# A recurrent recommender on one core: keys of eight steps gathered as whole rows and stored sorted, and seven sums moved from VectorE to GpSimd

## The chip, the core and the metric

The kernel runs on one core of one Trainium2 chip, in one launch. The metric is device time in microseconds, the median of three timed executions. Five engines work side by side and wait for each other only through semaphores: TensorE (PE in the profile) multiplies matrices, VectorE (DVE) and ScalarE (ACT) work elementwise, GpSimd (POOL) works elementwise more slowly and issues gathers, and SyncE (SP) issues plain transfers between the memory outside the core (DRAM in the code) and the core's own memory. Each engine takes its instructions strictly in the order of the program.

## What is computed

There are 1024 users, 100 time steps and 128 channels. Cut to what matters:

```
h[t]    = GRU(h[t-1], x[t])                         # 100 steps; keys[t] = h[t]
s[t]    = relu-MLP([key, item, key - item, key * item])   # one number per user and step
attn    = softmax over t of s[t], where mask[t] == 1
pooled  = sum over t of attn[t] * keys[t]           # 1024 users x 128 channels
a[t, b] = pooled.T[:100][t, b]                      # channel t of the pooled row is the weight of step t
g[t]    = AUGRU(g[t-1], keys[t], a[t])              # a second pass over the 100 steps:
          r, u = sigmoid(W [g, key]);  c = tanh(W [g * r, key]);  u = a[t] * u
          g    = (1 - u) * g + u * c
score   = MLP([user, item, history sum, item * history sum, g[length - 1]])
```

The second pass can only start once the pooled rows are there, and those need the last GRU step.

## The kernel before, in words

The users lie along the free dimension, 512 to a half, two halves; the 128 channels lie along the partitions. The **first phase** (`gru_phase`) loops over the 100 GRU steps. Per step and half TensorE runs the gate matmuls (L588) and the matmuls of the score MLP (L770). VectorE turns each new state by 32x32 blocks into the tile `kt` (L655), which holds four steps in a row layout, and `store` (L667) writes each such group of four to DRAM. GpSimd weighs the same tiles by the softmax weights and adds them up: product `kw` (L699), sum `pooled` (L700), and a rescaling of the sum (L689) when the softmax maximum moves on. The softmax goes by blocks of steps; each block's scores come from the rows `s_b`, which SP writes from the MLP's output `mv` (L825) and which VectorE reads (L865).

Between the phases lies a stretch that this document calls **the passage**: the last softmax blocks, the last sums, the product of the first AUGRU weights (L1114, L1122, L1128), the first AUGRU state `h_all` (L1137), and the rest of the pooled sums over channels 4 to 31 of each block (`rest`, L1141 for half 0 on GpSimd, L1143 for half 1 on VectorE). The pooled rows are then stored (L1146), gathered sorted by length (`gather_weights`, L1186), masked (L1206), turned, stored (L1216) and read back step by step as the tiles `at` (`load_att`, L1228).

The **second phase** (`augru_phase`) runs with the users sorted by length, longest first, so that later steps work on fewer columns. A step of a half is `half_step` (L1279): TensorE opens the three gates with the key's part (L1264) and closes them with the state's part (L1268); ScalarE applies sigmoid (L1292, L1293) and tanh (L1276); VectorE forms `r` (L1300), the weighted `u` (L1305, which reads `at`), `rest` (L1308) and the new state (L1298, L1302). The two halves alternate.

The keys must therefore come sorted. Before the change the keys of steps 0 to 3 are gathered as whole rows of one user (`keys_d[0]`, L158). All others lie in DRAM as rows of 32 channels by eight steps, 1 KB each, and one gather (`load_row`, L186, issued at L193) fetches 128 of these rows, so that a half takes 16 gathers for eight steps. Steps 4 to 11 of half 0 are gathered in the passage into the pool `kx` (four at step 98, four just after the loop, eight at the end of the passage); those of half 1 at the start of the second phase (16 gathers, four at once and twelve spread over steps 1 and 2). `load_key` (L1232) turns them back into the key tiles (L1253).

The order of the work is written out by hand: each engine's and each queue's order is the order of the program text. SP's transfers and GpSimd's gathers go to two queues (q1 and q0 in the profile) that share 16 DMA engines.

Of the kernel before, what the change touches and what calls it, by code (L numbers as in the profile page):

```python
# [9 lines left out]
F32 = mybir.dt.float32  # L10
# [9 lines left out]
P = 128  # L20
B = 1024
T = 100
HB = 512
# [4 lines left out]
R = 32  # L28
# [22 lines left out]

G = 4
WHOLE = 1
READ = [G] * WHOLE + [2 * G] * ((T - WHOLE * G) // (2 * G))
READ += [T - sum(READ)] * (sum(READ) < T)
FIRST = [sum(READ[:q]) for q in range(len(READ))]

# [28 lines left out]
def kernel(ctx: ExitStack, tc: tile.TileContext, a: dict, out: bass.AP):  # L86
# [30 lines left out]
    keys_d = [  # L117
        dram.tile([B, n * P] if q < WHOLE else [NK * P, n * R], F32, name=f"keys_d{q}")
        for q, n in enumerate(READ)
    ]  # L120
    mask_d = dram.tile([T, B], BF16, name="mask_d")
    inv_d = dram.tile([B, 3], I32, name="inv_d")
    kc_d = dram.tile([2, P], I32, name="kc_d")
# [43 lines left out]
    def load_rows(q, i, width, tiles):  # L167

        n = READ[q]
        if q < WHOLE:  # L170
            r = rows[q, i] = tiles.tile([P, GH, n * P], F32, tag="once", name="rows")
            for g in range(GH):
                gather(r[:, g, :], keys_d[q], g, i)
                yield
            return

        parts, tag = (2, "kt") if tiles is kx else (1, "rows")
        some = [
            tiles.tile([P, KH // parts, n * R], F32, tag=tag, name="rows") for _ in range(parts)
        ]  # L180
        rows[q, i] = some
        for k in range(-(-width // R)):
            load_row(q, i, k)
            yield

    def load_row(q, i, k):  # L186
        some = rows[q, i]
        part, at = divmod(k, KH // len(some))
        r = some[part]
        if later.get("pace") is not None:  # L190

            nc.gpsimd.tensor_copy(r[:, at, 0:1], later["pace"])  # L192
        nc.gpsimd.indirect_dma_start(  # L193
            out=r[:, at, :],
            out_offset=None,
            in_=keys_d[q],
            in_offset=bass.IndirectOffsetOnAxis(ap=idx_k[:, k, i : i + 1], axis=0),
        )

    def all_of(steps):  # L200
        for _ in steps:
            pass

    def gru_phase(pools):
# [334 lines left out]
        class Half:  # L539
# [125 lines left out]
                    self.store(q)  # L665

            def store(self, q):  # L667
                row, part = divmod(q - WHOLE, 2)
                nc.sync.dma_start(
                    out=keys_d[WHOLE + row].rearrange("(k p) m -> p k m", p=P)[  # L670
                        :, self.ks, ts(part, G * R)
                    ],
                    in_=self.kt[q].rearrange("p k n c -> p k (n c)"),
                )
# [259 lines left out]
        def gather_early(n):  # L934
            for _ in range(n):
                next(more_early)


        late, again, early_from = 6, 24, 84
        for s in range(T):  # L940
# [5 lines left out]
            def loads():  # L946
# [6 lines left out]
                if s == T - AHEAD:  # L953
# [107 lines left out]
        stage()  # L1061
        exponents()
        take(T + 1)
        some(4, 5)

        def key(n, half):
# [73 lines left out]
        kept = halves[0].kt[q]  # L1140
        halves[0].pool(T, nc.gpsimd, rest)  # L1141
        for half in halves:
            half.pool(T, nc.vector, rest)  # L1143
            to = pooled_d[half.cols, :].rearrange("(k r) f -> r k f", r=R)
            for p in range(P // R):
                nc.sync.dma_start(  # L1146
                    out=to[:, :, ts(p, R)], in_=pooled[ts(p, R), half.ks, :]
                )
        halves[0].kt[q] = kept
        halves[0].store(q)  # L1150
        all_of(more_early)

    def augru_phase(pools, widths, alive):

# [378 lines left out]
        def spread(q):  # L1533


            ahead = 3 if widths[FIRST[q]] > HB // 2 else 4
            n = NH * -(-widths[FIRST[q]] // R)
            return spread_over(n, NH * (FIRST[q] - FIRST[q - 1] + 1 - ahead))
# [161 lines left out]
```

## Time and profile before

| | |
|---|---|
| timed executions | 1998.15, 1998.83 and 1998.97 us; median 1998.83 us |
| the profiled execution, its own time | 2015.4 us |
| its span, first to last instruction | 2013.5 us |
| mean granted TensorE clock | 0.995 |
| TensorE busy | 1982.8 us (98% of the span) |
| VectorE busy | 1674.2 us (83%) |
| ScalarE busy | 940.4 us (47%) |
| GpSimd busy | 1262.1 us (63%) |
| gathers at L193 | 218, mean 972 ns on GpSimd |

A time in a row of the timeline or of the chain is counted from the start of the span. A row has its start, its length, the engine, the line of the kernel, the operation with what it writes and reads, and in square brackets how long the engine sat idle before it and what ended that. "issue" there means that nothing the profile shows ended it. The rows themselves stand in the prediction.

### The profile page before, as it was taken

Reading aid. Unit: us, or ns where it says so; the run is one execution under the profiler, and the core shown is the slowest. Engines: PE = TensorE matmul, PEld = TensorE weight load, DVE = VectorE, ACT = ScalarE, POOL = GpSimd, SP = SyncE. Lnnn points to the kernel's source line nnn. Section 1 sums busy time; section 2 is a strip of 40 time slices with the busy share of each in tenths; the row PEclk is TensorE's granted clock in tenths of the full one; section 3 lists DMA queues with packets and bytes.
Section 4 is the critical chain, followed back from the end, with each engine's and each line's share of the span. In section 5 each row is a group of like instructions: output and inputs, shape, how many; then the busy total and the mean of one; then the engine's idle time right before and its main releaser. Section 6 shows DMA issues by size and latency. Waiting matters only on the chain.

```text
span 2013.5 us, 40927 instructions
## 1 busy us (share of the span) xinstructions
PE 1982.8 (98%) x15324; PEld 875.7 (43%) x15324; DVE 1674.2 (83%) x3036; ACT 940.4 (47%) x1689; POOL 1262.1 (63%) x1300
## 2 busy tenths in 40 slices
PE   9999999999999999999999999999699999999998
PEld 2333333333333333333333333334244556678997
DVE  7888998887888897888888898998477777888885
ACT  4445444444445454445445454455234444445553
POOL 0333939569796959495987767989553354445331
PEclk9999999999999999999999999999899999999999
DMA  4443333323334334333432333332443333333331
GB/s 124 98 117 100 98 107 107 105 84 90 107 115 108 108 117 122 109 115 105 126 101 80 99 107 92 107 107 83 126 136 93 95 110 98 94 104 95 81 81 35
DMA packets 244572, 205.59 MB, mean 102 GB/s; under 512 B 61811, under 2 KB 207068, under 8 KB 244364
## 3 DMA queue, kind: packets, MB, share of 16 engines
q1 hardware_dynamic: 231852, 170.31, 29.9%
q0 software_dynamic: 12224, 32.05, 5.7%
q8 instruction: 122, 2.00, 0.4%
q14 instruction: 86, 0.70, 0.1%
q10 hardware_dynamic: 288, 0.52, 0.1%
HBM read 146.75 MB, written 54.42 MB: 100 GB/s over the span
## 4 chain that ended last, share of the span: by engine, by line
PE 93%; DVE 2%; POOL 2%; another core or an unknown queue 1%; ACT 1%; issue 1%; DMA 0%; SPq 0%; DVEq 0%; ACTq 0%; POOLq 0%
PE ps L588 48%; PE pm L770 17%; PE ph L1268 4%; PE pr L1268 4%; PE pu L1268 4%; PE ph L1264 4%; PE pr L1264 4%; PE pu L1264 4%; POOL pooled L700 1%; PE last L737 1%; POOL kw L699 1%; PE pr L1359 0%; PE ph L1359 0%; POOL hist L574 0%
## 5 line engine op out<-in xcount | busy, mean ns | idle before, releaser
L588 PE MATMUL ps<-x,wih 128*32 128x512 f32 x4800 | 601.9, 592 | 0.0
L588 PE MATMUL ps<-hn,whh 128*32 128x512 f32 x4752 | 596.8, 592 | 0.0
L588 PEld LDWEIGHTS ps<-x,wih 128*32 128x32 f32 x4800 | 174.4, 110 | 342.6 <-issue 337.9
L588 PEld LDWEIGHTS ps<-hn,whh 128*32 128x32 f32 x4752 | 172.8, 110 | 339.1 <-issue 337.0
L600 ACT ACTIVATE r<-ps,brz 128x512 f32<-128x512 f32 x200 | 137.5, 687 | 381.9 <-PE ps L588 381.7
L573 POOL TENSOR_TENSOR xm<-x,m 128x512 f32<-128x512 f32 x200 | 233.5, 1168 | 66.9 <-DMA m<-mask_d 66.6
L574 POOL TENSOR_TENSOR hist<-hist,xm 128x512 f32<-128x512 f32 x200 | 257.7, 1288 | 15.7
L193 POOL DMA_INDIRECT rows<-keys_d,idx_k x218 | 211.9, 972 | 85.2 <-POOL rows L192 49.7
L700 POOL TENSOR_TENSOR pooled<-pooled,kw 128x512 f32<-128x512 f32 x192 | 245.0, 1276 | 15.0
L699 POOL TENSOR_TENSOR kw<-kt,e 128x512 f32<-128x512 f32 x192 | 206.3, 1074 | 69.0 <-DVE e L888 69.0
L621 ACT ACTIVATE ps<-ps,bih 128x512 f32<-128x512 f32 x198 | 131.1, 662 | 229.8 <-DVE ps L618 228.7
L770 PE MATMUL pm<-hn,wk 128*32 128x512 f32 x1200 | 214.9, 592 | 0.0
L770 PE MATMUL pm<-kq,wkq 128*32 128x512 f32 x1200 | 214.8, 592 | 0.0
L1276 ACT ACTIVATE c<-ph,bh 128x510 f32<-128x510 f32 (+57 forms) x174 | 88.1, 506 | 254.5 <-PE ph L1268 222.1
L608 DVE SCALAR_TENSOR_TENSOR u<-ps,bhh,r 128x512 f32<-128x512 f32 x198 | 147.5, 745 | 68.8 <-PE ps L588 66.6
L770 PE MATMUL pm<-mv,w 128*32 128x512 f32 (+1 forms) x808 | 194.9, 592 | 1.0 <-DVE e L869 1.0
L192 POOL COPY rows<-rest 128x1 f32<-128x1 f32 x186 | 34.9, 188 | 209.5 <-DVE rest L1308 205.5
L631 DVE TENSOR_TENSOR d<-hn,ps 128x512 f32<-128x512 f32 x198 | 136.1, 687 | 35.9 <-ACT ps L621 35.5
L618 DVE TENSOR_TENSOR ps<-ps,u 128x512 f32<-128x512 f32 x200 | 140.0, 700 | 25.2 <-remote 4.1
L632 DVE TENSOR_TENSOR d<-ps,d 128x512 f32<-128x512 f32 x198 | 136.9, 691 | 26.1 <-ACT ps L622 11.1
L642 ACT COPY hn<-ps 128x512 f32<-128x512 f32 x198 | 115.5, 583 | 91.6 <-DVE kq L637 89.9
L1298 DVE TENSOR_TENSOR pu<-pu,c 128x510 f32<-128x510 f32 (+57 forms) x173 | 81.8, 473 | 89.7 <-ACT c L1276 62.9
(271 smaller groups left out, 3141.3 us busy)
## 6 DMA issues: line engine op xcount, KB each, us to landing
x<-in_hist_x SPq DMA_DIRECT2D x210, 256.0 KB
keys_d<-kt SPq DMA_DIRECT2D x48, 1024.0 KB
m<-mask_d SPq DMA_DIRECT2D x200, 128.0 KB
rows<-keys_d,idx_k POOLq DMA_INDIRECT x218
s_b<-mv SPq DMA_DIRECT2D x200, 8.0 KB
keys_d<-kt SPq DMA_DIRECT2D x32, 64.0 KB
mask_i<-in_mask SPq DMA_DIRECT2D x8, 200.0 KB
part_d<-part SPq DMA_DIRECT2D x2, 400.0 KB
```

What stands on the lines that cost most here:

```text
L193: nc.gpsimd.indirect_dma_start(out=r[:, at, :], out_offset=None, in_=keys_d[q], in_offset=bass.IndirectOffsetOnAxis(ap=idx_k[:, k, i : i + ...
L573: nc.gpsimd.tensor_mul(d, x, m)
L574: nc.gpsimd.tensor_add(acc, acc, d)
L588: nc.tensor.matmul(p[ts(q, R), :], lhsT=w[:, g, ts(q, R)], rhs=v, start=(j == 0), stop=(j == len(parts) - 1),)
L600: nc.scalar.activation(r, pr, AF.Sigmoid, bias=brz[:, 0:1])
L608: nc.vector.scalar_tensor_tensor(out=u, in0=ph, scalar=bhh[:, 2:3], in1=r, op0=ALU.add, op1=ALU.mult,)
L618: nc.vector.tensor_add(pi, pi, u)
L699: eng.tensor_mul(d, k, w)
L700: eng.tensor_add(acc, acc, d)
L770: nc.tensor.matmul(p[i][s, :], lhsT=w[:, s], rhs=v, start=start, stop=stop)
L1264: nc.tensor.matmul(p, lhsT=m[:, 1, :], rhs=k, start=True, stop=False)
L1268: nc.tensor.matmul(p, lhsT=m[:, 0, :], rhs=v, start=False, stop=True)
```

## The change

It touches three things. First, the keys of steps 4 to 11 are stored as whole rows of a user (`wide_d`, 8 steps by 128 channels, 4 KB a row) by four transfers of 32 partitions per half and group instead of one. At step 98, and again at the end of the loop, GpSimd gathers them sorted, 128 rows of 4 KB at a time, two gathers to a tile of `kx`, and SP stores each tile to `sorted_d`: two tiles a half, four in all. The key tiles are then loaded from there by plain transfers, four for each half and group of four steps: steps 4 to 7 at the end of the passage, steps 8 to 11 when the second phase reaches step 3. Second, the reading groups (`READ`) are therefore 4, 4, 4 and then 8 steps; the gathers of steps 12 and later stay as and when they were. Third, the rest sums of half 1 go to GpSimd.

```diff
-READ = [G] * WHOLE + [2 * G] * ((T - WHOLE * G) // (2 * G))
+WIDE = 3
+READ = [G] * WIDE + [2 * G] * ((T - WIDE * G) // (2 * G))
...
+    wide = sum(READ[WHOLE:WIDE])
+    wide_d = dram.tile([B, wide * P], F32, name="wide_d")
+    sorted_d = [dram.tile([HB, wide * P], F32, name=f"sorted_d{i}") for i in range(NH)]
...
+    def sort_rows(i):
+
+        pair = GH // 2
+        for part in range(GH // pair):
+            t = kx.tile([P, pair, wide * P], F32, tag="kt", name="sort")
+            for g in range(pair):
+                gather(t[:, g, :], wide_d, part * pair + g, i)
+            yield
+            nc.sync.dma_start(
+                out=sorted_d[i][ts(part, pair * P), :].rearrange("(g p) m -> p g m", p=P),
+                in_=t,
+            )
+
+    def load_sorted(q, i, tile):
+
+        n = READ[q] * R
+        rows[q, i] = [tile]
+        for p in range(P // R):
+            nc.sync.dma_start(
+                out=tile[ts(p, R)],
+                in_=sorted_d[i].rearrange("(k r) (p m) -> p r k m", r=R, p=P // R)[p][
+                    :, :, ts(q - WHOLE, n)
+                ],
+            )
...
             def store(self, q):
+                if q < WIDE:
+                    to = wide_d[self.cols, :].rearrange(
+                        "(k r) (p m) -> p r k m", r=R, p=P // R
+                    )
+                    for p in range(P // R):
+                        nc.sync.dma_start(
+                            out=to[p][:, :, ts(q - WHOLE, G * R)],
+                            in_=self.kt[q][ts(p, R)].rearrange("p k n c -> p k (n c)"),
+                        )
+                    return
...
-        more_early = load_rows(1, 0, HB, kx)
+        sort = [sort_rows(i) for i in range(NH)]
...
                 if last:
+                    all_of(sort[0])
                     nc.sync.dma_start(
                         out=q0[:R, :].rearrange("p (i f) -> p i f", i=NH),
...
             if s == T - 2:
-                gather_early(4)
+                next(sort[0])
+                next(sort[0])
...
-        gather_early(4)
+        next(sort[1])
+        next(sort[1])
         some(0, 1)
         take(T - 2)
...
         take(T + 1)
+        all_of(sort[1])
         some(4, 5)
...
         halves[0].pool(T, nc.gpsimd, rest)
         for half in halves:
-            half.pool(T, nc.vector, rest)
+            half.pool(T, nc.gpsimd, rest)
...
         halves[0].store(q)
-        all_of(more_early)
+        for half in halves:
+            load_sorted(WHOLE, half.i, kx.tile([P, KH, G * R], F32, tag="kt", name="rows"))
...
         sorted_rows = [gather_weights(i) for i in range(NH)]
-        ahead = load_rows(1, 1, widths[FIRST[1]], kp)
-        for _ in range(P // R):
-            next(ahead)
-        due = spread_over(-(-widths[FIRST[1]] // R) - P // R, NH * (FIRST[1] - 2))
+        ahead, due = iter(()), []
...
-            if t + 1 in FIRST[1:-1]:
+            if t + 1 == FIRST[WHOLE]:
+                for i in range(NH):
+                    tile = kp.tile([P, KH, G * R], F32, tag="rows", name="rows")
+                    load_sorted(WHOLE + 1, i, tile)
+            if t + 1 in (FIRST[WHOLE], *FIRST[WIDE:-1]):
                 all_of(ahead)
-                ahead, due = gathers(FIRST.index(t + 1) + 1), spread(FIRST.index(t + 1) + 1)
+                q = max(WIDE, FIRST.index(t + 1) + 1)
+                ahead, due = gathers(q), spread(q, t + 1)
```

More of the change, by code (lines that the diff above doesn't have):

```diff
@@ L119 @@
         for q, n in enumerate(READ)
+        if not WHOLE <= q < WIDE
     ]
+    keys_d[WHOLE:WHOLE] = [None] * (WIDE - WHOLE)
+    wide = sum(READ[WHOLE:WIDE])
+    wide_d = dram.tile([B, wide * P], F32, name="wide_d")
+    sorted_d = [dram.tile([HB, wide * P], F32, name=f"sorted_d{i}") for i in range(NH)]
     mask_d = dram.tile([T, B], BF16, name="mask_d")
@@ L175, in load_rows @@
             return
[L177 to L181, printed above, removed]
+        rows[q, i] = [tiles.tile([P, KH, n * R], F32, tag="rows", name="rows")]
         for k in range(-(-width // R)):
@@ L184, in load_rows @@
             yield
+    def sort_rows(i):
[19 more added lines that the diff above has]
+            )
     def load_row(q, i, k):
-        some = rows[q, i]
-        part, at = divmod(k, KH // len(some))
-        r = some[part]
+        r = rows[q, i][0]
         if later.get("pace") is not None:
-            nc.gpsimd.tensor_copy(r[:, at, 0:1], later["pace"])
+            nc.gpsimd.tensor_copy(r[:, k, 0:1], later["pace"])
         nc.gpsimd.indirect_dma_start(
-            out=r[:, at, :],
+            out=r[:, k, :],
             out_offset=None,
@@ L667, in store @@
             def store(self, q):
-                row, part = divmod(q - WHOLE, 2)
+                if q < WIDE:
[8 more added lines that the diff above has]
+                    return
+                row, part = divmod(q - WIDE, 2)
                 nc.sync.dma_start(
-                    out=keys_d[WHOLE + row].rearrange("(k p) m -> p k m", p=P)[
+                    out=keys_d[WIDE + row].rearrange("(k p) m -> p k m", p=P)[
                         :, self.ks, ts(part, G * R)
@@ L1531, in gathers, with spread @@
                 yield from load_rows(q, i, widths[FIRST[q]], kp)
-        def spread(q):
+        def spread(q, t):
             ahead = 3 if widths[FIRST[q]] > HB // 2 else 4
             n = NH * -(-widths[FIRST[q]] // R)
-            return spread_over(n, NH * (FIRST[q] - FIRST[q - 1] + 1 - ahead))
+            return spread_over(n, NH * (FIRST[q] - t + 1 - ahead))
         def spread_over(n, slots):
```

3 lines of the change are left out of this document (removed).

## The prediction

> **What bounds the kernel now.** I read the page first, then the chain of waits from 1360 us on, then the timeline of each engine around the passage.
>
> ```profile
> span 2013.5 us, 40927 instructions
> PE 1982.8 (98%) x15324; PEld 875.7 (43%) x15324; DVE 1674.2 (83%) x3036; ACT 940.4 (47%) x1689; POOL 1262.1 (63%) x1300
> PE   9999999999999999999999999999699999999998
> ```
>
> TensorE is busy 98% of the span. In the forty slices of its busy tenths there is one hole, the slice with a 6, which is 1409 to 1460 us: the passage and the first AUGRU steps. No line of the change touches a matmul, so it can win only what TensorE idles there. The chain of waits shows that idle time in two places.
>
> ```profile
> 1412.77 0.64 DVE last L699
> 1413.45 1.12 PE ph L1264 x2
> ...
> 1430.95 11.93 another core or an unknown queue
> 1443.48 2.91 another core or an unknown queue
> 1446.43 5.55 another core or an unknown queue
> ```
>
> The first is VectorE's rest sums, the second a stretch that the profile can't name. TensorE's timeline gives both in full:
>
> ```profile
> 1410.94 1.02 PE L1190 MATMUL row<-s_b,quad 128*128 128x512 f32 x2
> 1413.45 1.12 PE L1264 MATMUL ph<-hist,wh 128*128 128x510 f32 x2 [1.48 <-DVE last L699]
> ...
> 1433.07 1.01 PE L1268 MATMUL ph<-r,wh 128*128 128x506 f32 x2
> ...
> 1447.14 2.04 PE L1264 MATMUL pu<-k,wu 128*128 128x500 f32 x2 [9.68 <-issue]
> ...
> 1453.43 2.05 PE L1268 MATMUL ph<-r,wh 128*128 128x506 f32 x2 [3.40 <-DVE r L1300]
> ...
> 1461.00 0.60 PE L1213 MATMUL pw<-ident,att_r 128*96 128x128 f32 x4
> 1461.44 1.00 PE L1268 MATMUL ph<-r,wh 128*128 128x500 f32 x2
> ...
> 1466.45 1.00 PE L1268 MATMUL ph<-r,wh 128*128 128x500 f32 x2
> ```
>
> From 1461.44 to 1466.45 a half-step takes 5.01 us with TensorE never idle. From 1433.07 to 1461.44 there are two half-steps and two groups of transposes (L1213), whose spacing is 0.44 us (1461.00 to 1461.44). Undisturbed that is 2 x 5.01 + 2 x 0.44 = 10.9 us. It took 28.4, so 17.5 us are lost, and the releasers are unnamed.
>
> **How the profiled execution stands to the timed ones.** It took 2015.4 us by its own clock, 1.9 more than its span, and the median of the runs is 1998.83, so it is 16.6 us longer. Take the 17.5 us away and 1997.9 is left, 0.25 to 1.1 us under the three timed runs. Everything else in the span is a regular row of matmuls that has no room for 16 us of difference. I therefore hold the hole of 17.5 us to be of the profiled execution alone. The sum below is made against 2015.4 - 17.5 = 1997.9, and its difference is then put on 1998.83. That choice decides most of this forecast; its opposite is a rival below.
>
> **The change part by part.**
>
> *Rest sums.* VectorE does seven operations here after the first state (three products L699, three sums L700, one rescaling L689), and the last ends at 1414.05. GpSimd's rows for the same shape:
>
> ```profile
> 1413.43 0.62 DVE L700 TENSOR_TENSOR pooled<-pooled,last 128x448 f32<-128x448 f32 x1
> 1414.90 0.69 DVE L1300 TENSOR_TENSOR r<-h_all,pr 128x510 f32<-128x510 f32 x1 [0.86 <-issue]
> ...
> 1401.94 0.97 POOL L689 TENSOR_TENSOR pooled<-pooled,e 128x448 f32<-128x448 f32 x1
> 1402.88 1.02 POOL L699 TENSOR_TENSOR kw<-kt,e 128x448 f32<-128x448 f32 x1
> ...
> 1406.12 1.14 POOL L700 TENSOR_TENSOR pooled<-pooled,kw 128x448 f32<-128x448 f32 x1
> ```
>
> On GpSimd they follow its own at 1407.26 and take 3 x (1.02 + 1.14) + 0.97 = 7.45 us, to 1414.7, beside VectorE's work. TensorE's matmul for ph then starts where the one before it ends, and the 1.48 us of idle before 1413.45 go; VectorE's r, 1414.90 before, needs only ScalarE's sigmoid and no longer the sums. That is **-1.5 us**. It can't be more, since behind it TensorE is busy again; it is 0 if another wait stands there. The stores of half 1's pooled rows start 0.65 us later than before (1414.7 for 1414.05).
>
> *Stores of steps 4 to 11 and the key turns.* Sixteen transfers instead of four at steps 7 and 11. A transfer takes SP about 0.5 us (four pooled stores in 2.00 us, a row below), so 6 us more in two steps of GRU work of 13.7 us each, with inputs loaded two steps ahead: nothing. Without that lead a step would be up to 3 us late. VectorE's turns of the keys move the same elements: nothing.
>
> *Sorting in the passage.* Eight gathers of 512 KB take the place of 32 of 128 KB. GpSimd loses 24 issues, but they are not on TensorE's path. What is new stands in SP's queue: at the end of the loop the store of the third sorted tile is issued ahead of the scores' rows s_b, and it waits for two gathers. Behind it on SP stand the four s_b transfers for steps 96 and 97; VectorE's turn (L865) waits for them, and behind that the softmax, the last sums and the first weights.
>
> ```profile
> 1380.08 0.99 POOL L193 DMA_INDIRECT rows<-keys_d,idx_k  x1
> 1381.38 0.94 POOL L193 DMA_INDIRECT rows<-keys_d,idx_k  x1 [0.30 <-issue]
> ...
> L158 POOL DMA_INDIRECT rows<-keys_d,idx x8: 988/989/1007, 976.0 to 1018.6; - x8
> ...
> 977.80:978.80 1.00, 1.00 (x12) 0.29 (x8) 0.46 (x1) 0.55 (x1) 0.92 (x2) 1.00 0.74 234
> 1420.00:1421.40 1.40, 1.40 (x5) 0.26 (x3) 1.31 (x3) 0.58 (x1) 1.09 (x2) 1.00 1.17 352
> ...
> 1386.63 1.08 SPq L825 DMA_DIRECT2D s_b<-mv  x2
> ...
> 1388.47 0.73 DVE L865 STREAM_TRANSPOSE last<-s_b 128x512 f32<-128x512 f32 x1
> 1395.12 0.73 DVE L865 STREAM_TRANSPOSE last<-s_b 128x512 f32<-128x512 f32 x1 [0.22 <-DMA s_b<-mv]
> ...
> 1399.09 0.33 ACT L745 COPY part<-last 128x200 f32<-128x200 f32 x1 [0.40 <-PE last L737]
> ```
>
> The nearest gather (256 KB, issued at 976.0) has its data on the way until 978.8, at 234 GB/s; I take 2.7 us, and 1.1 more for the second 256 KB. The second gather of the pair is issued at 1381.38, so the pair is there at 1385.2, the store goes out, and the s_b transfers of step 97 follow near their old time of 1386.63. But 1 MB now lies ahead of them: 3.0 us at the 352 GB/s of the 1420 us row. An s_b transfer took 1.84 us (1386.63 to VectorE's start at 1388.47); the store ends at 1385.2 + 1.84 + 3.0 = 1390.0, and s_b just after, 1.6 us late. VectorE had 0.22 us of wait for s_b at 1395.12 and ScalarE 0.40 before 1399.09, which swallow part: **+1.0 us** for TensorE. Bounds: 0 if the gathers land 1.6 us sooner, +2.1 if the pair moves at 234 GB/s in full (1.05 MB in 4.5 us from 1381.9). The stores of the other tiles have nothing urgent close behind them.
>
> *Loading the sorted tiles.* At the end of the passage eight transfers, 2.1 MB, follow the pooled stores on SP's queue. Behind them come the store of the first weights (att_d) and the load of `at` for step 2, which VectorE's L1305 reads.
>
> ```profile
> 1414.08 2.00 SPq L1146 DMA_DIRECT2D pooled_d<-pooled  x4
> ...
> 1424.03 0.82 SPq L1228 DMA_DIRECT2D at<-att_d  x2
> ...
> 1431.39 0.68 DVE L1305 TENSOR_TENSOR pu<-pu,at 128x506 f32<-128x506 f32 x1
> ...
> 1432.71 0.55 DVE L1206 TENSOR_TENSOR att_r<-att_r,used_s 128x384 f32<-128x384 f32 x1
> ...
> 1421.80:1422.40 0.60, 0.60 (x5) 0.42 (x4) 0.42 (x1) 0.41 (x1) 0.30 (x1) 1.00 0.00 0
> ...
> 52.15 3.51 SPq L297 DMA_DIRECT2D mask_i<-in_mask  x4
> ...
> 55.00:58.50 3.50, 3.50 (x38) 1.05 (x34) 2.06 (x3) 2.82 (x5) 0.00 (x0) 1.00 1.01 178
> ```
>
> Half 1's pooled stores started at 1414.08; they now start at 1414.7 + 1.4 (the late s_b on GpSimd's sums) = 1416.1, 2.0 later. The queue's data then ended by 1421.6 (full rate until 1421.4, nothing after 1421.8), now 1423.6. For 2.1 MB in pieces of 512 bytes to 32 partitions the nearest row is mask_i: pieces of 400 bytes to 32 partitions, 178 GB/s. If a piece costs the same, that is 228 GB/s and 9.2 us; the bounds are 6.0 us at 352 and 11.8 at 178. I take 9.2, since that row has the shape of these loads. With 0.5 MB of weight gathers on the same engines (1.5 us) the queue is free at 1434.3; about 0.5 us for the small store and 2.5 for the load (1.84 as for s_b, 0.7 for 253 KB) give 1437.3. L1305 stood at 1431.39, and TensorE needs the next r at 1433.07 + 5.01 + 0.44 = 1438.5; five VectorE operations (three of about 0.7, one of 0.55, r itself 0.68) take 3.3 us, so L1305 may wait until 1435.2, and 1434.7 once the two terms above have moved everything by -0.5. That leaves **+2.6 us**, with bounds 0 and +5.2.
>
> The Trainium skill, page "DMA: Bandwidth & Descriptors", section "Queues, rings and completion order", says that on each DMA engine the descriptors of one queue are consumed in ring order. The trace agrees as far as it goes: the store issued at 1416.12 still moved data until 1421.6, behind the pooled stores.
>
> The loads of steps 8 to 11 at step 3 lie ahead of the weights of step 4 on the same queue, but those are read two half-steps later than they could be (10 us): nothing; if that lead were gone, another 9 us.
>
> *The 16 gathers of half 1.* They leave the start of the second phase.
>
> ```profile
> 1429.58 0.95 POOL L193 DMA_INDIRECT rows<-keys_d,idx_k  x1 [0.30 <-issue]
> 1448.34 0.94 POOL L193 DMA_INDIRECT rows<-keys_d,idx_k  x1 [0.30 <-issue]
> ...
> 1466.76 0.71 DVE L1253 STREAM_TRANSPOSE k<-rows 128x512 f32<-128x512 f32 x1
> ```
>
> The key turn that needs them is at 1466.76, which is 1449.3 without the hole; the last is issued at 1448.34. So a timed run may wait a little here: between -1.1 us (all that the timed runs lie above 1997.9) and 0. I take 0, since TensorE has the spare time of a half-step before it uses that key.
>
> **The sum** is -1.5 + 1.0 + 2.6 + 0 = +2.1 us, so **2000.9 us**. All low ends give 1998.83 - 1.5 - 1.1 = 1996.2, all high ends 1998.83 + 0 + 2.1 + 5.2 = 2006.1.
>
> **The rivals.** *The hole is in the timed runs too* and comes from the 16 gathers. For it: it starts 1.4 us after the first of them and ends soon after the last. Against it: sixteen gathers just as close went before, without a hole, and the 16.6 us between profile and median would have to come from elsewhere. If so, the change removes it: 1998.83 - 17.5 + 2.1 = 1983.4.
>
> *Slower: the loads go at half rate.* The place is L1305 of step 2, half 0; the price is what `at` comes later than 1434.7. Two rows speak for it: 178 GB/s into 32 partitions, 352 for transfers over 128. At 176 GB/s the loads take 11.9 us, `at` comes at 1440.0, and the time is 1998.83 - 1.5 + 1.0 + 5.3 = 2003.6. It counts as slower from a load time of 11.1 us up. Against it: with 512 bytes a piece costs less for each byte.
>
> The Trainium skill, page "SBUF — State Buffer", section "Door 1: The DMA port swizzle", says that 32 neighbouring partitions reach 8 of the 16 ports, hence half the rate; by that rule this rival is the forecast, and the two rates agree with it.
>
> *The loads aren't felt.* If a load of 512-byte pieces runs at 352 GB/s, `at` comes in time, and -1.5 + 1.0 = -0.5 is left: 1998.3.
>
> **How the numbers follow.** Forecast 0.57, half rate 0.21, loads not felt 0.14, hole 0.08. What a measurement can tell from no change is about 0.2%, 4.0 us: 1994.8 to 2002.8. The forecast's own spread passes 2002.8 in about one case of eight; half rate is mostly above, loads not felt inside, the hole below. That gives faster 0.09, same 0.66, slower 0.25. The range 1995.5 to 2005.0 leaves out the hole below and the far end of the half rate above.
>
> **What would show it.** Right: TensorE's idle before L1264 in the passage is gone; L865 waits for s_b by 1 to 3 us, behind SP's store; SP's load of `at` is 10 us or more behind the pooled stores, with L1305 waiting for it; TensorE's row of step 2 has a gap of 2 to 3 us. Wrong: a time under 1990, which would make the hole a cost of the timed runs; no wait at L865 or L1305; or a new gap outside 1380 to 1460 us.

## The result, and the profile after

| | before | changed |
|---|---|---|
| median of the timed executions | 1998.49 us (six, 1996.03 to 1998.97) | 2009.92 us (six, 2008.54 to 2010.93) |
| ratio | | 1.0056, interval 1.0044 to 1.0068 |
| the profiled execution, its own time | 2015.4 us | 2010.49 us |

The changed kernel is slower by 11.4 us (8.8 to 13.6 by the interval). The forecast was 2000.9 us, slower by 2.1, with a range up to 2005.0.

The page of the changed kernel, with its span, the busy time of each engine and TensorE's tenths in forty slices, and then the view of what TensorE waited for from 1385 to 1480 us (total, times, longest):

```profile
span 2008.7 us, 40934 instructions
PE 1986.3 (99%) x15324; PEld 1502.1 (75%) x15324; DVE 1667.6 (83%) x3021; ACT 941.3 (47%) x1689; POOL 1246.9 (62%) x1283
...
PE   9999999999999999999999999999999999999998
```

```profile
PE pr L1300 <- DVE k L1289: 5.0, 1, 5.0
PE pw L1249 <- issue: 2.9, 1, 2.9
PE pm L805 <- ACT mv L855: 2.7, 1, 2.7
PE pk L1282 <- ACT att_t L1235: 0.7, 1, 0.7
PE ph L1304 <- DVE r L1336: 0.5, 1, 0.5
```

The slice with a 6 is gone, and so is the wait of 1.48 us ahead of the first ph matmul. Three new waits stand in their place. (Lines have moved by 35 or 36: L805 was L770, L1300 was L1264, L1304 was L1268.) The chain of waits says what is behind them:

```profile
1386.30 4.88 DMA s_b<-mv
1391.21 0.05 issue
1391.26 0.69 ACT mv L855
...
1438.84 3.40 DMA at<-att_d
1442.33 0.70 DVE pu L1341
...
1458.49 11.21 DMA att_d<-att_t
1469.71 3.38 DMA at<-att_d
1473.18 0.69 DVE pu L1341
...
1475.32 2.01 PE pr L1300 x2
```

All three end in a transfer of SP's queue. The queue itself, first one row of before, then of the changed kernel (start, time to issue, what, how many):

```profile
1379.00 12.02 SPq L825 DMA_DIRECT2D s_b<-mv  x6
```

```profile
1385.22 0.36 SPq L196 DMA_DIRECT2D sorted_d<-sort  x1
1385.67 7.38 SPq L860 DMA_DIRECT2D s_b<-mv  x6
...
1421.40 9.05 SPq L206 DMA_DIRECT2D rows<-sorted_d  x8
1430.65 0.82 SPq L1236 DMA_DIRECT2D att_d<-att_t  x1
1438.84 0.82 SPq L1264 DMA_DIRECT2D at<-att_d  x2
...
1450.84 7.54 SPq L206 DMA_DIRECT2D rows<-sorted_d  x8
1458.49 1.85 SPq L1252 DMA_DIRECT2D att_d<-att_t  x1
1469.71 8.80 SPq L1264 DMA_DIRECT2D at<-att_d  x8
```

The score rows of step 96, issued at 1379.00 before, leave at 1385.67: SP stood at the store of the third sorted tile until its gathers were there. Twice a store of weights (att_d) goes out behind eight loads of sorted keys, and SP can issue the load of `at`, which reads what that store writes, only 8.2 and 11.2 us later (1430.65 to 1438.84, 1458.49 to 1469.71). The windows of the changed kernel (busy time of each engine, then the granted clock, the share of the DMA engines and GB/s) show the rates and one thing more:

```profile
1422.00:1425.00 3.00, 3.00 (x7) 0.68 (x6) 2.48 (x5) 1.51 (x3) 1.56 (x2) 1.00 1.14 345
1427.00:1438.00 11.00, 10.34 (x31) 4.49 (x30) 1.98 (x3) 4.41 (x7) 4.65 (x5) 1.00 1.18 194
...
1390.00:1395.00 5.00, 3.01 (x7) 1.05 (x8) 3.31 (x10) 1.82 (x4) 1.61 (x2) 0.68 0.21 74
1395.00:1400.00 5.00, 5.00 (x19) 3.89 (x17) 3.34 (x13) 1.58 (x3) 2.94 (x3) 0.64 0.25 97
...
1445.00:1450.00 5.00, 4.55 (x7) 2.06 (x8) 4.92 (x9) 1.33 (x2) 0.00 (x0) 0.66 0.20 65
1475.00:1480.00 5.00, 4.68 (x6) 2.19 (x7) 4.45 (x8) 0.00 (x0) 2.63 (x5) 0.50 0.71 229
```

The first row is the plain store of 1 MB from 128 partitions, at 345 GB/s. The second is the loads into 32 partitions each, 194 GB/s together with the gathers of the weights. The last four are TensorE's clock at and after its waits of 2.7, 2.9 and 5.0 us: as a mean of five microseconds it is 0.50 to 0.68, so a wait costs more than its length.

TensorE's row has 15324 matmul records in every kernel here, and from record 12800 on they stand in the same order, so a stage can be timed from one record to another by their numbers in the row. For the profiled executions (us; "last steps" is where few users are left):

| stage (records) | before | changed | no_gathers_2 | rest_only | rest_only_2 | stores_late_2 | loads_wide | loads_later | all_later_2 |
|---|---|---|---|---|---|---|---|---|---|
| score rows (12840 to 12880) | 7.59 | 13.86 | 7.59 | 7.68 | 7.59 | 7.59 | 12.20 | 14.40 | 7.59 |
| first weights (to 12930) | 14.35 | 14.35 | 14.34 | 14.35 | 14.35 | 16.00 | 14.35 | 14.35 | 14.82 |
| AUGRU step 1 (to 12996) | 26.37 | 24.66 | 26.37 | 36.94 | 24.66 | 24.66 | 24.66 | 24.66 | 24.66 |
| step 2 (to 13030) | 29.16 | 17.31 | 11.77 | 27.33 | 11.77 | 18.23 | 11.77 | 11.77 | 11.77 |
| step 3 and on (to 13100) | 28.83 | 36.65 | 28.83 | 28.83 | 39.52 | 36.17 | 28.83 | 28.83 | 28.83 |
| last steps (14470 to 15140) | 94.4 | 90.6 | 90.6 | 96.9 | 91.0 | 90.6 | 94.2 | 96.1 | 90.6 |

Undisturbed, the five stages are 7.59, 14.35, 24.66 (26.37 with the sums on VectorE), 11.77 and 28.83. So the change pays 6.3 us for the score rows, 5.5 for the first loads and 7.8 for the second, and wins 1.7 with the sums.

### The profile page after: what moved, and what is told of

It reads as the page before. It is cut to its first block, busy times and chain, and to the rows that moved or that the text cites. A ratio compares the mean times of both kernels' runs of the same rounds, so it can differ in the third digit from the quotient of the medians.

```text
span 2008.7 us, 40934 instructions
## 1 busy us (share of the span) xinstructions
PE 1986.3 (99%) x15324; PEld 1502.1 (75%) x15324; DVE 1667.6 (83%) x3021; ACT 941.3 (47%) x1689; POOL 1246.9 (62%) x1283
## 4 chain that ended last, share of the span: by engine, by line
PE 97%; DMA 1%; DVE 1%; ACT 0%; issue 0%; ACTq 0%; DVEq 0%
PE ps L613 51%; PE pm L805 18%; PE ph L1304 4%; PE pr L1300 4%; PE ph L1300 4%; PE pu L1300 4%; PE pr L1304 4%; PE pu L1304 4%; PE last L772 1%; DMA att_d<-att_t 1%; PE pr L1395 0%; DMA at<-att_d 0%; PE ph L1395 0%; DMA s_b<-mv 0%; PE p L1515 0%
## 5 line engine op out<-in xcount | busy, mean ns | idle before, releaser
L613 PE MATMUL ps<-x,wih 128*32 128x512 f32 x4800 | 696.1, 593 | 0.0
L613 PE MATMUL ps<-hn,whh 128*32 128x512 f32 x4752 | 690.4, 592 | 0.0
L613 PEld LDWEIGHTS ps<-x,wih 128*32 128x32 f32 x4800 | 408.7, 110 | 109.2 <-issue 38.3
L613 PEld LDWEIGHTS ps<-hn,whh 128*32 128x32 f32 x4752 | 407.0, 110 | 104.9 <-issue 37.4
L599 POOL TENSOR_TENSOR hist<-hist,xm 128x512 f32<-128x512 f32 x200 | 258.1, 1291 | 15.7
L735 POOL TENSOR_TENSOR pooled<-pooled,kw 128x512 f32<-128x512 f32 (+1 forms) x195 | 248.8, 1276 | 15.3
L734 POOL TENSOR_TENSOR kw<-kt,e 128x512 f32<-128x512 f32 (+1 forms) x195 | 209.1, 1072 | 68.0 <-DVE e L923 68.0
L805 PE MATMUL pm<-hn,wk 128*32 128x512 f32 x1200 | 245.7, 592 | 0.0
L805 PE MATMUL pm<-kq,wkq 128*32 128x512 f32 x1200 | 245.6, 592 | 0.0
L218 POOL DMA_INDIRECT rows<-keys_d,idx_k x186 | 181.4, 975 | 75.7 <-POOL rows L217 70.6
L805 PE MATMUL pm<-mv,w 128*32 128x512 f32 (+1 forms) x808 | 199.1, 597 | 2.7 <-ACT mv L855 2.7
```

Source lines behind the costliest of these rows:

```text
L218: nc.gpsimd.indirect_dma_start(out=r[:, k, :], out_offset=None, in_=keys_d[q], in_offset=bass.IndirectOffsetOnAxis(ap=idx_k[:, k, i : i + ...
L599: nc.gpsimd.tensor_add(acc, acc, d)
L613: nc.tensor.matmul(p[ts(q, R), :], lhsT=w[:, g, ts(q, R)], rhs=v, start=(j == 0), stop=(j == len(parts) - 1),)
L734: eng.tensor_mul(d, k, w)
L735: eng.tensor_add(acc, acc, d)
L805: nc.tensor.matmul(p[i][s, :], lhsT=w[:, s], rhs=v, start=start, stop=stop)
```

## The experiments

The theory is that these four terms come from the order on SP and on VectorE, and that the 16 removed gathers had a cost of their own before. The rivals are the sizes of the prediction, contention for the DMA engines instead of order, small pieces instead of few partitions, and a hole that belongs to one execution.

The runs fell on four chips, one for each comparison, and the kernel before did not take the same time on all of them, so a run is only compared with the kernel before beside it: 2019.23 us (rest_only, stores_late, loads_wide, loads_later), 2013.56 (again, all_later, no_gathers, later_vector), 1998.80 (all_later_2 and the three plus16 runs), 1998.22 (no_gathers_2, plus16_2, stores_late_2, rest_only_2).

### The sums alone: rest_only and rest_only_2

```diff
-            half.pool(T, nc.vector, rest)
+            half.pool(T, nc.gpsimd, rest)
```

> The kernel before with one line changed: the rest sums of half 1 on GpSimd. Queue theory (the changed kernel lost 6.1 us to the score rows behind a store on SP, 5.4 and 7.9 us to the two groups of loads ahead of the AUGRU weights, and won 1.5 us from the sums): 1998.5 - 1.5 = 1997.0, TensorE's 1.48 us of idle ahead of its ph matmul in the passage gone. Rival, the sums just wait elsewhere: 1998.5. On the hole of 17.5 us in the profile of before: if it belongs to that one execution, the profile here, which keeps the 16 unpaced gathers, has none and its own time is near 1997; if the gathers make it, the profile shows it again and the timed runs contain it.

> The kernel before with the rest sums of half 1 on GpSimd, again. Where before takes 1998: 1.5 to 1.8 us less, 1996.8; where it takes 2013 to 2019: more than before, as in the first trial (the gathers then follow each other without a break of 2.4 us, and the hole grows). Rival, the gathers' longer row costs on any chip: 1998.5 or more.

Measured: 2029.19 us beside 2019.23, ratio 1.0049 (1.0033 to 1.0064), and 2003.39 beside 1998.22, 1.0026 (1.0016 to 1.0036). Slower both times, by two different things. On the first chip the hole is there again in the profile, and every timed execution is as long (2025.7 to 2030.8). In this timeline of rest_only ScalarE copies the key of a turn that TensorE had finished at 1444.97:

```profile
1443.91 1.06 PE L1246 MATMUL pk<-ident,rows 128*128 128x128 f32 x4
...
1462.50 0.57 ACT L1247 COPY k<-pk 128x500 f32<-128x500 f32 x1 [16.91 <-remote]
...
1463.71 2.03 PE L1264 MATMUL pu<-k,wu 128*128 128x500 f32 x2 [13.41 <-ACT c L1276]
```

17.5 us lie between the end of the turn and the copy, which reads nothing but its result. On the second chip the same copy follows within 0.1 us, and the wait is another one, VectorE's key turn for the last of the gathers, with TensorE's clock at half behind it (the last row is a window):

```profile
1430.50 0.60 PE L1246 MATMUL pk<-ident,rows 128*128 128x128 f32 x4
...
1431.14 0.58 ACT L1247 COPY k<-pk 128x500 f32<-128x500 f32 x1 [2.32 <-PE pk L1246]
...
1453.56 0.95 POOL L193 DMA_INDIRECT rows<-keys_d,idx_k  x1 [0.30 <-issue]
...
1456.54 0.71 DVE L1253 STREAM_TRANSPOSE k<-rows 128x512 f32<-128x512 f32 x1 [9.36 <-DMA rows<-keys_d,idx_k]
...
1457.31 2.02 PE L1264 MATMUL pr<-k,wr 128*128 128x496 f32 x2 [7.72 <-DVE k L1253]
...
1455.00:1460.00 5.00, 2.69 (x4) 1.22 (x5) 3.43 (x6) 0.00 (x0) 4.17 (x7) 0.50 0.38 107
```

The sums on GpSimd put off its gathers, and the key turn pays: TensorE's row wins 1.7 us in step 1 (26.37 to 24.66) and loses 10.7 in step 3 (39.52 for 28.83). So the edit only helps where the 16 gathers are gone.

### The gathers left out: no_gathers and no_gathers_2

```diff
+        if (q, i) == (1, 1):
+            nc.gpsimd.memset(some[0], 0.0)
         for k in range(-(-width // R)):
-            load_row(q, i, k)
+            if (q, i) != (1, 1):
+                load_row(q, i, k)
```

> The kernel before without the 16 gathers of half 1 for steps 4 to 11: GpSimd fills their tile with zeros instead, so the keys of these steps are left out and everything else is done. If the unbroken row of gathers makes the hole, the profile has no hole, TensorE's row from its ph matmul at 1413 us to the third AUGRU step is regular, and the time is 17 to 20 us under before where before takes 2018, some 6 where it takes 1998. Rival, the hole has another cause: the same time as before.

> The kernel before without the 16 gathers of half 1 for steps 4 to 11 again (their tile is filled with zeros, these keys are left out), on whatever chip it falls. Theory that the gathers' cost is one of the chip: where before takes 2013 to 2019, 14 to 20 us under before, as in the first trial; where before takes 1998, 1996 to 1997, that is 1 to 3 us under it. Rival: 14 us under before on any chip.

Measured: 1999.14 beside 2013.56, ratio 0.9927 (0.9914 to 0.9941), 14.4 us; and 1994.01 beside 1998.22, 0.9980 (0.9971 to 0.9989), 4.2 us. What TensorE waits for from 1385 to 1480 us in no_gathers is what before has too, without the hole:

```profile
PE ph L1267 <- DVE last L702: 1.5, 1, 1.5
PE pk L1249 <- issue: 0.7, 1, 0.7
PE pu L1101 <- ACT hist L1076: 0.3, 1, 0.3
```

The hole goes with the 16 gathers, and they cost 4.2 us even where there is no such hole. Between 1 and 3 had been expected there. That the 4.2 us are a wait of the key turn, as in rest_only_2, is inferred: no profile of the kernel before from such a chip was kept.

### The store behind the score rows: stores_late and stores_late_2

```diff
-        pair = GH // 2
+        pair, tiles = GH // 2, []
...
-            yield
+            tiles.append(t)
+            yield
+        for part, t in enumerate(tiles):
             nc.sync.dma_start(
```

> The changed kernel with both stores of a half's sorted tiles issued together at the later of their two places, so that no store stands on SP ahead of the score rows of steps 96 to 98; all else as changed. Queue theory: the 2.7 us of TensorE idle at 1392 us and what follows it are gone, 6.1 us: 2009.9 - 6.1 = 2003.8. Rival, the size of the prediction (1.0 us): 2008.9. Rival, the loss is a contention of the gathers and the stores for the DMA engines and not the order on SP: 2009.9.

> The changed kernel with both stores of the sorted tiles behind the score rows, again. Where before takes 1998, the changed kernel took 2009.9: 2003.7 by the 6.2 us of TensorE's stages; where before takes 2013 to 2019, 2009 to 2012 as in the first trial. Rival, the size of the prediction: 2008.9 where before takes 1998.

Measured: 2011.81 beside 2019.23, ratio 0.9967 (0.9956 to 0.9979), and 2005.93 beside 1998.22, 1.0037 (1.0024 to 1.0051). The stage of the score rows is back to 7.68 and 7.59. Against the changed kernel's 2009.92 (before at 1998.49) the second is 4.0 us less, not 6.2: 1.65 us come back in the next stage (16.00 for 14.35), where TensorE waits 1.5 us for a copy of ScalarE, and 0.9 in step 2. The same order takes 14.57 in that stage in stores_late and 14.82 in all_later_2, so the cause of the 1.65 stays open. The 2003.8 expected of stores_late was worked out from a time on another chip, and the changed kernel was not run beside it.

### The changed kernel again, where before takes longer: again

> The changed kernel itself, beside the other three on one chip, since the kernel before took 1998.5 us in the first comparison and 2019.2 in that of the last four kernels. By stages of TensorE's row the change costs 6.2 (score rows) + 5.5 + 7.8 (two groups of loads) - 1.7 (sums) = 17.8 us, less what the 16 gathers cost before. If that gather cost differs from chip to chip and the rest doesn't, then where before takes 2018 to 2020 the changed kernel takes 2010 to 2016, faster than before, and where before takes 1998 it takes 2010. Rival, chips differ in all by the same amount: 11 us over before on any chip.

Measured: 2014.34 us beside 2013.56, ratio 1.0006 (0.9997 to 1.0015): no difference. The gap between the two kernels is not one number; it depends on what before's gathers cost on the chip. A second reading concerns the score rows. TensorE waits 2.4 us there, nearly as long as the 2.7 of the first profile, but its clock stays whole (the view of waits, then the windows):

```profile
PE pm L805 <- ACT mv L855: 2.4, 1, 2.4
...
1390.00:1395.00 5.00, 2.64 (x14) 1.35 (x13) 1.99 (x5) 1.58 (x3) 3.37 (x3) 1.00 0.34 135
1395.00:1400.00 5.00, 5.00 (x31) 4.14 (x28) 4.62 (x19) 2.87 (x7) 1.59 (x2) 1.00 0.45 166
```

The stage takes 10.59 us and not 13.86, so about half of the 6.3 us is the clock. At the same place waits of 2.2, 2.7 and 2.8 us (loads_wide, the changed kernel, loads_later) were followed by a clock of 0.66, 0.64 and 0.50, and this one of 2.4 us was not, so the length of the wait alone does not decide. The Trainium skill, page "TensorE: Matmul & The Clock Gate", section "Part 1: The HAM clock gate (the "warmup" mystery)", says that the clock is halved after an idle window of some 3.4 us, and that the window runs freely. By that rule none of these waits is long enough to fill a window, so the page and the measurement differ in the length; that equal waits can end either way would fit a window that runs freely.

### The loads over 128 partitions: loads_wide

```diff
-                out=tile[ts(p, R)],
-                in_=sorted_d[i].rearrange("(k r) (p m) -> p r k m", r=R, p=P // R)[p][
-                    :, :, ts(q - WHOLE, n)
+                out=tile[:, ts(j, part)],
+                in_=sorted_d[i].rearrange("(k r) (p m) -> (r p) k m", r=R, p=P // R)[
+                    :, ts(j, part), ts(q - WHOLE, n)
```

> The changed kernel with the loads of the sorted tiles cut otherwise: each of the four transfers of a tile writes 128 partitions and a quarter of the columns, not 32 partitions and all of them; the same bytes in the same 512-byte pieces, but the rows land at other partitions, so the keys of steps 4 to 11 are not those of the reference (no work is left out). Theory that 32 partitions halve the rate: the loads run near 350 GB/s and not 178, each group is done some 6 us sooner, the first group's 5.4 us go and 6 of the second's 7.9: 2009.9 - 11.4 = 1998.5. Rival, the small pieces are what is slow in this direction: 178 GB/s again and 2009.9.

Measured: 2002.59 beside 2019.23, ratio 0.9925 (0.9911 to 0.9940). The same stretch of the loads, in the changed kernel and here:

```profile
1426.00:1433.00 7.00, 6.33 (x18) 2.54 (x18) 0.55 (x1) 2.49 (x5) 5.34 (x6) 1.00 1.18 185
```

```profile
1426.00:1433.00 7.00, 6.26 (x19) 2.50 (x18) 0.03 (x1) 2.64 (x5) 5.47 (x6) 1.00 1.14 297
```

In this stretch the queues move 1.6 times as much. The 2.1 MB of the loads alone, in the same 512-byte pieces, take 9.0 us and not 12.8 by the times of their packets (1425.3 to 1434.3, 1425.0 to 1437.8), and both stages are whole again (11.77, 28.83) although the loads stand where they stood. The small pieces are not what is slow; the cut by partitions is, or the order in which it reads the pieces from DRAM, which changed with it. The Trainium skill's rule that 32 neighbouring partitions reach half of the 16 ports (page "SBUF — State Buffer", section "Door 1: The DMA port swizzle") agrees with the first of these.

### The loads at other places: loads_later

```diff
-        for half in halves:
-            load_sorted(WHOLE, half.i, kx.tile([P, KH, G * R], F32, tag="kt", name="rows"))
...
                 store_chosen(1, pa.tile([P, HB], F32, tag="a", name="spare"))
+                for n in range(NH):
+                    load_sorted(WHOLE, n, kx.tile([P, KH, G * R], F32, tag="kt", name="rows"))
...
-                for i in range(NH):
-                    tile = kp.tile([P, KH, G * R], F32, tag="rows", name="rows")
-                    load_sorted(WHOLE + 1, i, tile)
+                wait = [kp.tile([P, KH, G * R], F32, tag="rows", name="rows") for i in range(NH)]
...
+                if i == 0 and t in (FIRST[WHOLE], FIRST[WHOLE] + 1):
+                    load_sorted(WHOLE + 1, t - FIRST[WHOLE], wait.pop(0))
```

> The changed kernel with the same loads at other places of SP's order: the first group behind the loads of the weights of steps 2 and 3, the second group's two tiles in steps 4 and 5 behind weights already loaded ahead. Queue theory: no weight waits behind a load, 5.4 + 7.9 us go: 2009.9 - 13.3 = 1996.6, with the loads still at 178 GB/s. Rival, the loads hold up the weights wherever they stand because they fill the DMA engines: 2004 or more, with waits for the weights of step 4.

Measured: 2006.76 beside 2019.23, ratio 0.9938 (0.9924 to 0.9952). The first group's loads are as slow as in the changed kernel (12.8 us by their packets, in a window of 204 GB/s), and yet both stages are whole (11.77, 28.83), with TensorE busy all through:

```profile
1436.00:1445.00 9.00, 9.00 (x29) 4.42 (x28) 6.55 (x11) 3.03 (x5) 0.00 (x0) 1.00 1.13 204
```

So the order on SP's queue is what costs, and the rate only sets how much; either remedy is enough. The time lies where the rival had it (2004 or more), but the waits of the rival are not there. The expected 1996.6 was worked out from a time on another chip. Here the wait for the score rows was 2.8 us with the clock down (14.40), and the last steps took 5.5 us more than in the changed kernel's profile.

### All of it together: all_later, later_vector and all_later_2

> The changed kernel with both stores of the sorted tiles behind the score rows, the first loads behind the weights of steps 2 and 3, and the second loads in steps 4 and 5: the two edits stores_late and loads_later together. Queue theory: 6.2 + 5.5 + 7.8 = 19.5 us less than the changed kernel beside it. Rival, the two savings overlap or come back in the last steps, where the kernels of the last call lost up to 5 us: 13 to 15 us less.

> The kernel all_later with the rest sums of half 1 back on VectorE. Queue theory: 1.5 us more than all_later, the idle time ahead of the first ph matmul of the AUGRU back. Rival, with the sums on GpSimd the pooled rows and all behind them come later, so VectorE is as good or better: the same time or less.

> The kernel all_later again, as the base of the three that follow and against before on a further comparison. Theory: 1998.6 us as in the last call, give or take 5 for the chip, whether before takes 1998 or 2018, since it has neither the 16 gathers nor the waits on SP; so it is faster than before by 4 to 20 us. Rival, what it won was of one chip: within 2 us of before.

Measured: all_later 1998.64 beside 2013.56, ratio 0.9926 (0.9913 to 0.9940), 15.7 us under the changed kernel beside it (2014.34); all_later_2 1994.59 beside 1998.80, 0.9981 (0.9972 to 0.9990). With these transfers moved in SP's order the change is faster than before on both chips, by 14.9 and 4.2 us. What TensorE still waits for in all_later_2 from 1385 to 1480 us:

```profile
PE pk L1282 <- ACT att_t L1235: 0.7, 1, 0.7
PE first L1165 <- DVE s_b L1161: 0.3, 1, 0.3
PE pu L1135 <- ACT hist L1110: 0.3, 1, 0.3
```

With the sums back on VectorE (later_vector) it took 1999.32, 0.7 more; the stage of step 1 is 26.52 for 24.66, but the times' intervals overlap, so the sums show in TensorE's row and not in the time. The expected 19.5 us became 15.7 because the score rows cost only 3.0 in the run beside it (10.59 for 7.62).

### Gathers added: plus16, plus16_2, plus16_thin and plus16_gap

```diff
+        spare = [kp.tile([P, KH, G * R], F32, tag="rows", name="spare16") for _ in range(2)]
+        for k in range(KH):
+            to = spare[k // 8][:, 2 * (k % 8) : 2 * (k % 8) + 2, :].rearrange("p k m -> p (k m)")
+            nc.gpsimd.indirect_dma_start(
+                out=to[:, :256],
+                out_offset=None,
+                in_=keys_d[WIDE],
+                in_offset=bass.IndirectOffsetOnAxis(ap=idx_k[:, k, 1:2], axis=0),
+            )
```

> The kernel all_later with 16 gathers of 128 rows of 1 KB added on GpSimd right behind the gathers of the pooled rows, where the kernel before had its own; what they fetch is read by nobody. Theory that an unbroken row of gathers delays TensorE's signals: ScalarE and VectorE wait for matmuls that ended long before, TensorE's row of the second and third AUGRU steps has a hole of 10 to 18 us, and the time is 14 to 20 us over all_later where before takes 2013 to 2019, 4 to 6 where it takes 1998. Rival, the hole before came from a dependency of its gathers or from SP's order: the time of all_later.

> The kernel all_later with 16 gathers added whose rows nobody reads. Where before takes 1998: 1996.5 again, no hole, only the wait of 1.9 us of the key turn for its late load. Where before takes 2013 to 2019: if gathers delay TensorE's signals there, a hole of 10 to 18 us as in before, 2008 to 2016; if it takes something of before's order as well, under 2003.

> As plus16, with rows of 128 bytes instead of 1 KB: as many gathers and rows, an eighth of the bytes. If the number of rows or the issuing on GpSimd makes the hole, it is as long as in plus16; if the bytes make it, it is gone or under 3 us.

> As plus16, with four small fills on GpSimd ahead of each added gather, so that the gathers stand about 2.5 us apart and not 1.25. If it takes an unbroken row of gathers, there is no hole and the time is that of all_later, up to 3 us more; if each gather costs a share, whatever its distance, the hole is spread out and the time is that of plus16.

Measured: beside 1998.80, where all_later_2 took 1994.59, plus16 took 1996.49 (ratio 0.9991, 0.9982 to 1.0000), plus16_thin 1995.26 (0.9982, 0.9973 to 0.9991) and plus16_gap 2013.80 (1.0082, 1.0068 to 1.0096); plus16_2 took 1996.87 beside 1998.22 (0.9992, 0.9983 to 1.0001). Both comparisons were on chips where before takes 1998, and there is no hole there; plus16 takes 1.9 us over all_later_2, and 4 to 6 had been expected. What plus16 shows is the load of the sorted keys, late beside the gathers' bytes; with an eighth of the bytes the wait is gone (step 3 and on: 32.71 in plus16, 28.83 in thin). Timeline of plus16:

```profile
1450.99 0.71 DVE L1289 STREAM_TRANSPOSE k<-rows 128x512 f32<-128x512 f32 x1 [3.68 <-DMA rows<-sorted_d]
```

The gap run did not answer its question. The fills stretch GpSimd's work until 1472, and a column copy behind it (L219), which paces later gathers, reads a tile that VectorE wants to write:

```profile
1472.48 0.19 POOL L219 COPY rows<-rest 128x1 f32<-128x1 f32 x1
...
1475.60 0.67 DVE L1344 SCALAR_TENSOR_TENSOR rest<-pu,h_all 128x496 f32<-128x496 f32 x1 [19.77 <-POOL rows L219]
```

Whether 16 gathers in the changed order make a hole on a chip where before takes 2013 or more was not seen.

## Why the prediction was wrong, step by step

Three terms of the sum carry the miss, and all three stand in the order of SP's queue: the score rows (+6.3 us for +1.0), the first loads (+5.5 for +2.6) and the second loads (+7.8 for nothing). In none of them was there a price for TensorE's half clock, although two rows of the prediction's own timeline show it (pairs of matmuls of 2.04 and 2.05 us, at 1447.14 and 1453.43, for 1.00).

**The hole as a thing of the profiled execution alone: wrong, and nearly the right base by luck.** The execution profiled for before (2015.4 us) is none of the timed ones, which had no such hole in the first comparison. Elsewhere timed executions have it too (the profile of rest_only is of one): where before takes 2013.56 us, leaving the gathers out wins 14.4 of them. It goes with the chip or with the moment; each chip was seen in one comparison only, so the two are not told apart. The base was off in two more places that cancel: the profiled execution also had 3.8 us more in the last steps (94.4 for 90.6), and the timed ones paid 4.2 for the gathers. 2015.4 - 17.4 (29.16 to 11.77) - 3.8 = 1994.2, which is the 1994.0 of no_gathers_2, and 4.2 more is 1998.4, near the median. The step that failed is "everything else in the span is a regular row of matmuls that has no room": one subtraction that came out within 1 us was taken for proof.

**The 16 gathers of half 1, "I take 0, since TensorE has the spare time of a half-step": wrong, it is -4.2 us.** rest_only_2 shows how little the spare time is: of 9.36 us of VectorE's wait TensorE feels 7.72, and then the half clock. This was the one gain that the prediction did not count.

**The sums, -1.5 us: right.** The stage is 1.7 us shorter, and the wait is gone.

**The store ahead of the score rows, +1.0 us with bounds of 0 and 2.1: the path to TensorE was wrong, 6.3 us.** The place was right (VectorE's turn of s_b waits behind the store, for 4.4 us), and the store went out at 1385.22, as worked out (1385.2), in part by luck: its gathers were issued 1.4 us earlier and took as much longer. But the working set the store against the rows of step 97, due at 1386.63, and followed them through VectorE. Those of step 96, due at 1379.00, stand behind the same store and leave 6.7 us late. ScalarE needs them too, since it can't write the next `mv` until they have been read, and TensorE's next matmuls read that `mv`. Before, ScalarE had only 0.24 us of wait there; the first row is of before, the others of the changed kernel:

```profile
1389.22 1.26 ACT L820 ACTIVATE mv<-pm,bm 64x512 f32<-64x512 f32 x2 [0.24 <-PE pm L770]
...
1391.26 1.26 ACT L855 ACTIVATE mv<-pm,bm 64x512 f32<-64x512 f32 x2 [3.69 <-DMA s_b<-mv]
1391.45 0.73 DVE L900 STREAM_TRANSPOSE last<-s_b 128x512 f32<-128x512 f32 x1 [4.36 <-DMA s_b<-mv]
```

2.7 us of idle time and about 3 us of half clock follow in TensorE's row.

**The loads ahead of `at`, +2.6 us with bounds of 0 and 5.2: mis-sized, 5.5 us.** The chain was right: at the load of `at`, TensorE's gap is 2.9 and 0.5 us, near the forecast (2 to 3). Three inputs were off. By their packets the 2.1 MB took 12.8 us (1425.0 to 1437.8, 164 GB/s) beside the gathers of the weights; 9.2 and 1.5 for those gathers were taken. They started 1.4 us later than worked out, because the late score rows had put off GpSimd's sums and so the pooled stores. And the small store and the load behind them took 4.5 us to the start of VectorE's operation (1437.8 to 1442.33), not 3.0. What no term held is the half clock behind the gap, most of the other 2.1 of the 5.5 us.

**The loads of steps 8 to 11, "nothing; if that lead were gone, another 9 us": wrong, 7.8 us.** The lead of two half-steps, 10 us, was counted against the loads alone. What stands behind them is a store of weights and then the load that reads it, 11.2 + 3.4 us in the chain, longer than the lead. TensorE waits 5.0 us, and most of the rest is again the clock (0.50 from 1475 to 1480).

**The stores of steps 4 to 11 and the turns, nothing: right.** The stage up to record 12840 is 1385.3 us after and 1386.7 before.

The terms as measured: -1.7 + 6.3 + 5.5 + 7.8 - 4.2 = +13.7 us, against 11.4 measured (8.8 to 13.6). The 2.3 us between can be found by comparing with no_gathers_2: 0.9 lie in the rest of the two profiled rows, where the changed kernel is ahead (0.7 of it before record 12840), 1.1 between these two profiled executions and the medians of their runs, and 0.3 between the two comparisons' times of before. Of the rivals, "the loads go at half rate" had the rate nearly right, by the row of 178 GB/s (164 measured), and its 2003.6 falls short because it priced one place of three. "The hole is in the timed runs" holds on other chips, and there too the change doesn't win: in the profile of again the stages pay 3.0 + 0.5 + 5.8 + 7.3 - 1.7 = 14.8 us (10.59, 14.80, 17.58 and 36.11 for 7.61, 14.35, 11.77 and 28.83, and 24.66 for 26.37), against the 14.4 that no_gathers wins beside it, and the ratio is 1.0006.

## What to carry to other kernels

A transfer put into a queue delays everything behind it, so list all that stands behind, with the time at which each was due before, and not only the nearest; where a store and the load that reads it follow, their two latencies add to the delay. A wait of TensorE of 2 us or more may cost its length twice, by the clock: here waits of 2.2, 2.7 and 2.8 us did, and one of 2.4 us did not. And loads cut along 32 partitions at a time took 12.8 us here where the same bytes cut over all 128 took 9.0, so cut along the columns where the layout allows it, or place the load where nothing waits behind it.

## What the runs showed that was not expected

The same kernel took 1998 us on some chips and 2013 to 2019 on others, and most of the difference lies in one place: while GpSimd issues gathers 1.25 us apart, ScalarE and VectorE start 2.5 to 17.5 us after the matmul that they wait for has ended (rest_only, 1444.97 to 1462.50 at the longest), and on other chips within 0.1 us (rest_only_2, 1431.10 to 1431.14). On the former the last steps, which have gathers too, also take 94 to 97 us and not 91. Leaving out 16 gathers removes the hole, but not the longer last steps (95.5 in no_gathers). Why the chips differ, and what carries the signal so late, stays open; that it is the number of gathers in a row rather than their bytes was not settled, since no run with added gathers fell on such a chip.
